# A two-layer graph attention kernel: the target's own row enters the early sums in the first stage, and the shared last blocks get four buffers

## The chip, the cores and the metric

The kernel runs on one core of one Trainium2 chip. The metric is the device time of one execution in microseconds; the kernel before has a median of 1749.48 us over 3 runs (1748.37 to 1754.7).

## What is computed

Two graph attention layers over the same sparse graph of 3327 nodes with 1024 features, each followed by a residual sum and a layer norm. Layer 0 has 8 heads of 128 columns, layer 1 has one head of 1024.

```python
# layer 0; layer 1 is the same with one head, its own W, and a relu on the result
h = (x @ W).reshape(C, H, D)
e = leaky_relu(alpha_src[:, :, None] + alpha_dst[:, None, :], 0.2)
attn = softmax(where(adj[None] == 0, -inf, e), axis=-1)
x = layernorm(x + einsum('hij,jhd->ihd', attn, h))
```

The adjacency is drawn with a density of 0.0024 and made symmetric, and every node is its own neighbour too. The weight exp(leaky_relu(s+d)) is computed as max(exp(0.8 s) exp(d), exp(0.2 d)); the factor exp(0.2 s) that is left out is the same for all edges of a target and falls out in the division. So a target row is a weighted sum of the rows of its neighbours, divided by the sum of the weights. The node's own edge is handled apart from the listed neighbours.

## The kernel before

**Tiles and tables.** The nodes make 26 tiles of 128 targets (NT = 26). The first stage multiplies x by W0 tile by tile and stores a table `h0_d` in memory: for each node 8 heads of 129 columns (128 and a one, which gathers the sum of weights: 1032 columns, DW) and 16 columns of exponentials (1048 in all, HW0). Beside the matmuls it turns the adjacency into lists of edges: masks come in as bytes (`ads`, three buffers), `count` and `words` count and pack them, `listing` finds the columns and writes `idx` and `tgt`, the source and target of each edge. The edges of a target tile are laid out in 17 lists of 128: blocks 0 and 1 of four lists each hold sources in the first 13 tiles, blocks 2 and 3 the others, and block 4 (EB) one list that all groups share, the "shared last block".

**The first stage's second half.** From tile 13 on a generator `sums_so_far` (L675) runs between the matmuls. It takes the first 20 target tiles (EARLY = 20) and does for each the sums over blocks 0 and 1 alone. For a block it fetches four lists with indirect transfers issued by POOL (`fetch`, L691) into one of three buffers (`near`, `near`, `far`), computes `w` and the weights `e` on VectorE (L708 to L712) and adds 64 small matmuls into PSUM (L721). After both blocks ScalarE copies the three PSUM banks to `z` (L764) and SyncE stores them as `half_d[s]` (L765).

**What orders the first stage.** Everything is scheduled by hand. The projection calls `pace()` after every two k-steps (12 slots for a tile of x); each slot lets `counting`, `listing` and `sums_so_far` take their next steps. The instructions stand in each engine's queue in the order in which the program emits them. In `sums_so_far` the weights of the next block are emitted ahead of the copy of the banks (L764).

**Layer 0 (the second stage).** `Layer0` items follow: 20 early targets with the blocks 2, 3 and 4 and 6 late ones with 0 to 4, in the order 20, 0 to 4, 21, 5 to 9 and so on. `prepare` (L1072, L1075) loads the node's own row `own` from `h0_d` and, for early targets, the stored sums `half`. `own` (L1081 to L1083) computes the own edge's weight on VectorE, `scale_own` (L1090) multiplies the own row by it with 8 ScalarE instructions, and `sums` (L1121) adds `own` and `half` to PSUM by matmuls with the identity, three for each row. `gather` (L1032) takes its buffers from two free lists: five for blocks of four lists and two (`ends`) for the shared last blocks. The requests stand in one fixed order, and `send` stops at the first one that has no free buffer.

**Layer 1 (the third stage).** `Target` items gather rows of `y_d` in the same way, sum them (L1234), turn the result (`finish`, tile `xT`) and multiply it by W1 (L1266).

Of the kernel before, what the change touches and what calls it, by code (L numbers as in the profile page):

```python
# [9 lines left out]
F32 = mybir.dt.float32  # L10
BF16 = mybir.dt.bfloat16
U8 = mybir.dt.uint8
I32 = mybir.dt.int32
# [13 lines left out]
def kernel(  # L27
# [111 lines left out]

    def by_head(row):  # L140
        return row[:, :DW].rearrange("p (h d) -> p h d", h=H)

    class Rows:

# [390 lines left out]
    with ExitStack() as own, tc.manual_schedule():  # L535
# [16 lines left out]

        def load_mask(t):
            if t < NT:
                ads[t] = masks[t % 3]
                if t == NT - 1:
                    nc.vector.memset(ads[t].bitcast(I32), 0)
                    nc.vector.memset(ads[t][:, :1], 1.0)
                for r in pieces(t):
                    nc.gpsimd.dma_start(ads[t][r, :N], adj[at(t, r), :])  # L560
# [114 lines left out]

        def sums_so_far():

            acc = part.bank("L", [P, 3, HALF], "part")
            acc = acc[:, :, : 3 * DH1].rearrange("p n (h d) -> p n h d", h=3)
            src = [near[0], near[1], far]  # L680
            k = EARLY * HB % 3
            src = src[-k:] + src[:-k] if k else src
            bound = nc.gpsimd.to_reg(THR - 1)

            def fetch(n):
                s, b = divmod(n, HB)
                if s > EARLY:
                    return
                for g in range(NG):
                    k = b * NG + g  # L690
                    nc.gpsimd.indirect_dma_start(  # L691
                        out=src[n % 3][:, g, :], out_offset=None, in_=h0_d[:THR, :],
                        in_offset=bass.IndirectOffsetOnAxis(ap=idx[:, s, k : k + 1], axis=0),
                        bounds_check=bound, oob_is_err=False,
                    )

            def marks(s):
                oh = part.sbuf("oh", [P, HB * NG, GT], 2)
                nc.vector.tensor_tensor(
                    oh, io_t[:, :GT].unsqueeze(1).to_broadcast([P, HB * NG, GT]),  # L700
                    tgt[:, s, : HB * NG].unsqueeze(2).to_broadcast([P, HB * NG, GT]), OP.is_equal,
                )
                return oh

            def weights(val, b, re, oh):
                blk = slice(b * NG, (b + 1) * NG)
                w = part.sbuf("w", [P, NG, H], 4)
                nc.vector.tensor_tensor(w, val[:, :, DW : DW + H], re[:, blk, :], OP.mult)  # L708
                nc.vector.tensor_tensor(w, w, val[:, :, DW + H :], OP.max)
                e = part.sbuf("e", [P, H * P], 2).rearrange("p (g h t) -> p g h t", g=NG, h=H)  # L710
                wide = [P, NG, H, GT]
                nc.vector.tensor_tensor(  # L712
                    e, oh[:, blk, :].unsqueeze(2).to_broadcast(wide), w.unsqueeze(3).to_broadcast(wide), OP.mult
                )
                return e

            def sums(acc, val, b, e, heads_):
                vals = val[:, :, :DW].rearrange("p g (h d) -> p g h d", h=H)
                for h in heads_:
                    for g in range(NG):  # L720
                        nc.tensor.matmul(  # L721
                            acc[g * GT : (g + 1) * GT, h // 3, h % 3, :], e[:, g, h, :], vals[:, g, h, :],
                            start=b == 0 and h in HEADS, stop=b == HB - 1 and h + 1 in HEADS,
                        )

            def listed(s):
                re = part.sbuf("re", [P, HB * NG, H], 3)
                nc.sync.dma_start(re, re_d[s][:, : HB * NG, :])
                return re

            res = [listed(0), listed(1)]
            for _ in range(3):
                yield
            for n in range(2):
                fetch(n)
                yield
                yield
                yield
            oh = marks(0)
            fetch(2)  # L740
            yield
            e = weights(src[0], 0, res[0], oh)
            yield
            for s in range(EARLY):
                for b in range(HB):
                    n = s * HB + b
                    val, last = src[n % 3], b == HB - 1
                    if n:
                        fetch(n + 2)
                    yield  # L750
                    if last and s + 1 < EARLY:
                        oh = marks(s + 1)
                    yield
                    sums(acc, val, b, e, range(H // 2))
                    yield
                    sums(acc, val, b, e, range(H // 2, H))
                    if last:
                        res.pop(0)
                    if n + 1 < EARLY * HB:
                        e = weights(src[(n + 1) % 3], (b + 1) % HB, res[0], oh)  # L760
                z = part.sbuf("z", [P, DW], 1)
                for n in range(3):
                    nh = HEADS[n + 1] - HEADS[n]
                    nc.scalar.activation(by_head(z)[:, HEADS[n] : HEADS[n + 1], :], acc[:, n, :nh, :], AF.Copy)  # L764
                nc.sync.dma_start(half_d[s], z)  # L765
                if s + 2 < EARLY:
                    res.append(listed(s + 2))
                yield

        wt = pool.tile([P, KT, WW], F32, bufs=1, name="wt")  # L770
        arow = [near[1][:1, 2 + n, :D] for n in range(2)]
# [12 lines left out]
        for n in range(4):  # L784
            half = slice(n % 2 * HALF, (n % 2 + 1) * HALF)
            nc.tensor.matmul(avs[:, n, :], one, arow[n // 2][:, half], start=True, stop=True)
        masks = [pool.tile([P, NP], U8, bufs=1, name=f"ad{n}") for n in range(3)]
        for ad in masks:
            nc.vector.memset(ad[:, N:], 0.0)
        junk = pool.tile([P, THR], U8, bufs=1, name="junk")  # L790
# [32 lines left out]
        score_column(7)  # L823
        opening.close()
        ph.more_banks(own, "late", {"S": 1})
        part.more_banks(own, "part", {"L": 1})
        ph.xp = bank("S", [P, EB, XS], "xp")
        ph.dd = ph.xp[:, 0, NG * NX :]

# [49 lines left out]
        for t in range(3, NT):  # L879
            load_x(t + 3)  # L880
            if 4 <= t < 4 + KT:
                nc.sync.dma_start(wt1[:, t - 4, :], w1[(t - 4) * P : (t - 3) * P, :])
            if t == 12:
                n, own_a = NT - 1, pool.tile([P, NT], I32, bufs=1, name="own")
                nc.vector.memset(own_a[:, n:], 0)
                step, m = adj.ap[0][0] + 1, rows(n)
                nc.sync.dma_start(
                    own_a[:, :n], bass.AP(tensor=adj.tensor, offset=adj.offset, ap=[[step, P], [P * step, n]])
                )
                nc.sync.dma_start(  # L890
                    own_a[:m, n:], bass.AP(tensor=adj.tensor, offset=adj.offset + n * P * step, ap=[[step, m], [1, 1]])
                )
            if t == 11:
                ph.iota([P, P], [[1, P]], "io_t", base=1, dst=io_t)
            if t == 16:
                nc.gpsimd.tensor_copy(loop, own_a)
            if t in (9, 10):
                table, w = (h0_d, HW0) if t == 9 else (y_d, HW)
# [73 lines left out]
    def sparse(own):  # L972
# [1 line left out]
        pool, bank, sbuf = ph.pool, ph.bank, ph.sbuf  # L974
        NS = 5
        srcs = near + [pool.tile([P, NG, HG], F32, bufs=1, name=f"src{n}") for n in range(HB, NS)]
        ends = [pool.tile([P, 1, HG], F32, bufs=1, name=f"end{n}") for n in range(2)]
        r1 = Rows(pool, 1)
        grow = pool.tile([P, NT], F32, bufs=1, name="grow")
        grows = pool.tile([P, NT, H], F32, bufs=1, name="grows")  # L980
# [74 lines left out]
        class Layer0:  # L1055
# [10 lines left out]
            def prepare(self):  # L1066
# [2 lines left out]
                self.y = ys[self.n % 3]  # L1069
                load_rows(self.y[:, :D], x, self.t)  # L1070
                self.h = sbuf("own", [P, HW0], 2)
                nc.sync.dma_start(self.h, h0_d[self.t * P : (self.t + 1) * P, :HW0])  # L1072
                if self.t < EARLY:
                    self.half = sbuf("xT", [P, DW], 2, "half")
                    nc.sync.dma_start(self.half, half_d[self.t])  # L1075

            def own(self):

                t, h = self.t, self.h
                es = self.es = sbuf("es0", [P, H], 2)  # L1080
                nc.vector.tensor_tensor(es, grows[:, t, :], h[:, DW : DW + H], OP.mult)  # L1081
                nc.vector.tensor_tensor(es, es, h[:, DW + H :], OP.max)
# [2 lines left out]
            def scale_own(self):  # L1085

                h = self.h
                for n in range(H):
                    d = slice(n * DH1, (n + 1) * DH1)
                    nc.scalar.activation(h[:, d], h[:, d], AF.Copy, scale=self.es[:, n : n + 1])  # L1090

# [22 lines left out]
            def sums(self, b):  # L1114
# [1 line left out]
                rowsof = self.src.pop(b)[:, :, :DW].rearrange("p g (h d) -> p g h d", h=H)  # L1116
                j = self.blocks.index(b)
                for n in self.banks.get(j, ()):
                    for row in (self.h, self.half) if self.t < EARLY else (self.h,):
                        part = row[:, HEADS[n] * DH1 : HEADS[n + 1] * DH1]  # L1120
                        nc.tensor.matmul(  # L1121
                            self.acc[n].rearrange("p h d -> p (h d)"), ident, part, start=False, stop=False
                        )
                if b == EB:
                    for h in range(H):
                        nc.tensor.matmul(
# [48 lines left out]
        class Target:  # L1175
# [80 lines left out]
            def finish(self):  # L1256

                t, z, res = self.t, self.z, self.res
                xT = sbuf("xT", [P, DW], 2)[:, :D].rearrange("p (k q) -> p k q", k=KT)
                yield from ph.transposed(xT, z, (0, 1))  # L1260
                o = sbuf("z", [P, D], 3, "o")
                for g in range(2):
# [283 lines left out]
```

## Time and profile before

| | |
|---|---|
| median of 3 runs | 1749.48 us |
| the profiled execution | 1751.44 us, its span 1749.6 us |
| TensorE, VectorE, ScalarE, GpSimd busy | 86%, 65%, 28%, 60% |
| transfers | 596.13 MB, mean 341 GB/s |
| first stage, up to the last projection matmul | to 563 us |
| first to last copy of the early sums (L764) | 274.8 to 562.9 us |
| layer 0 | to about 1060 us |
| layer 1 | to the end |

PE is TensorE, PEld its weight loads, DVE VectorE, ACT ScalarE, POOL GpSimd, SP SyncE. The page of the profile gives totals and 40 slices of 43.7 us. Other views give a stretch of time in numbers: busy us of each engine (with its instructions), the TensorE clock granted as a share of full speed, the mean busy share of the 16 DMA engines (it can exceed 1, because packets overlap), and GB/s. A wait is put down to what came last. A matmul in float32 leaves two records.

### The profile page before, as it was taken

The numbers are of one execution on the slowest core, as the hardware profiler recorded it, in microseconds if no ns is written. First come the engines' busy times: TensorE is split into PE (matmuls) and PEld (weight loads), VectorE is DVE, ScalarE is ACT, GpSimd is POOL, SyncE is SP. The second block draws the span as 40 slices with busy tenths as digits, with TensorE's granted clock in tenths as the row PEclk, the third lists the DMA queues.
The fourth block names the chain that finished last, engine by engine and source line by source line (L and its number), as shares of the span: only waits on it lengthen the run. The fifth ranks groups of instructions, "written<-read, shape, count | busy, mean of one in ns | idle before, by whom it ended". The sixth has DMA issues, their size and how long they took to land.

```text
span 1749.6 us, 34204 instructions
## 1 busy us (share of the span) xinstructions
PE 1497.3 (86%) x12755; PEld 865.2 (49%) x12755; DVE 1143.2 (65%) x3126; ACT 494.6 (28%) x1424; POOL 1050.7 (60%) x1309
## 2 busy tenths in 40 slices
PE   9799989898998477676676664799999999999998
PEld 5566655565665355555555542344444444444443
DVE  6799998888886788676877765344444453444443
ACT  5677752232323133332332322011111011111110
POOL 5433155776775666555656666677667766676750
PEclk9999999999999699887888886899999999999999
DMA  7688988999999999999999999999999999999980
GB/s 186 123 157 164 185 232 305 316 388 348 360 346 355 371 410 412 398 396 384 396 396 386 390 384 383 359 401 393 396 399 386 394 392 387 388 394 410 386 336 36
DMA packets 190321, 596.13 MB, mean 341 GB/s; under 512 B 37914, under 2 KB 47924, under 8 KB 190146
## 3 DMA queue, kind: packets, MB, share of 16 engines
q0 software_dynamic: 131056, 459.23, 73.4%
q1 hardware_dynamic: 58932, 134.36, 20.5%
q8 instruction: 103, 1.69, 0.4%
q14 instruction: 72, 0.59, 0.1%
q10 hardware_dynamic: 158, 0.26, 0.0%
HBM read 593.70 MB, written 54.99 MB: 371 GB/s over the span
## 4 chain that ended last, share of the span: by engine, by line
PE 41%; DMA 17%; DVE 5%; issue 2%; POOL 1%; ACT 0%; DVEq 0%; SPq 0%; ACTq 0%; POOLq 0%
PE mm L1266 22%; PE acc L1234 13%; DMA src<-h_d,idx 7%; DMA own<-h_d 4%; PE acc L1134 3%; DMA near<-h_d,idx 2%; PE acc L1121 2%; DMA src<-y_d,idx 2%; DVE e L1108 2%; PE tr L203 1%; DVE pr L998 1%; DVE y L1151 1%; DMA end<-h_d,idx 1%; DMA av<-in_L_gnn_a_dram 1%; DMA half<-half_d 0%
## 5 line engine op out<-in xcount | busy, mean ns | idle before, releaser
L571 PE MATMUL mm<-wt,xT 128*128 128x384 f32 (+1 forms) x1248 | 415.3, 478 | 0.4 <-DMA xT<-in_x_t_dram 0.4
L1266 PE MATMUL mm<-wt,xT 128*128 128x512 f32 x832 | 387.6, 604 | 0.0
L1032 POOL DMA_INDIRECT src<-y_d,idx x248 | 251.4, 1014 | 122.6 <-PE acc L1234 48.2
L571 PEld LDWEIGHTS mm<-wt,xT 128*128 128x128 f32 x1248 | 230.7, 195 | 130.2 <-issue 36.0
L1266 PEld LDWEIGHTS mm<-wt,xT 128*128 128x128 f32 x832 | 149.7, 189 | 198.9 <-issue 194.0
L1269 DVE SCALAR_TENSOR_TENSOR o<-mm,y 128x512 f32<-128x512 f32 x52 | 35.9, 691 | 317.3 <-PE mm L1266 317.3
L1032 POOL DMA_INDIRECT src<-h_d,idx x152 | 160.2, 1054 | 108.3 <-PE acc L1134 24.8
L1032 POOL DMA_INDIRECT near<-y_d,idx x168 | 171.1, 1018 | 65.7 <-issue 21.7
L1134 PE MATMUL acc<-src,e 128*32 128x129 f32 x2432 | 103.4, 340 | 74.6 <-DVE e L1108 74.6
L691 POOL DMA_INDIRECT near<-h_d,idx x112 | 124.1, 1108 | 51.5 <-issue 23.9
L1032 POOL DMA_INDIRECT near<-h_d,idx x96 | 103.3, 1076 | 75.5 <-DMA src<-h_d,idx 28.6
L1234 PE MATMUL acc<-src,es 128*32 128x341 f32 x1488 | 124.8, 470 | 26.0 <-DVE es L1225 26.0
L1134 PEld LDWEIGHTS acc<-src,e 128*32 128x32 f32 x2432 | 86.8, 138 | 92.6 <-DVE e L1108 81.2
L1248 ACT ACTIVATE z<-y,ri 128x342 f32<-128x342 f32 (+1 forms) x78 | 39.5, 569 | 299.1 <-DVE ri L1244 299.1
L1134 PE MATMUL acc<-near,e 128*32 128x129 f32 x1664 | 68.8, 332 | 58.6 <-DVE e L1108 44.2
L1108 DVE TENSOR_TENSOR e<-oh,way 128x1024 f32<-128x1024 f32 x90 | 109.9, 1221 | 7.9 <-PE acc L1134 0.6
L206 ACT ACTIVATE xT<-tr 128x512 f32<-128x512 f32 x52 | 31.0, 597 | 236.0 <-PE tr L203 236.0
L1134 PEld LDWEIGHTS acc<-near,e 128*32 128x32 f32 x1664 | 57.8, 134 | 70.7 <-DVE e L1108 48.6
L1234 PEld LDWEIGHTS acc<-src,es 128*32 128x32 f32 x1488 | 43.1, 112 | 96.3 <-issue 43.9
L1121 PE MATMUL acc<-own,ident 128*128 128x387 f32 (+1 forms) x156 | 72.0, 547 | 16.7 <-ACT own L1090 16.7
L411 ACT ACTIVATE junk<-ad 128x1664 uint8<-128x1664 uint8 x52 | 83.0, 1595 | 7.6 <-POOL ad L400 6.1
L1234 PE MATMUL acc<-near,es 128*32 128x342 f32 (+1 forms) x1008 | 82.0, 458 | 1.5 <-DVE es L1225 1.5
(225 smaller groups left out, 2378.7 us busy)
## 6 DMA issues: line engine op xcount, KB each, us to landing
own<-h_d SPq DMA_DIRECT2D x26, 524.0 KB
y_d<-y SPq DMA_DIRECT2D x26, 514.0 KB
y<-y_d SPq DMA_DIRECT2D x26, 514.0 KB
xT<-in_x_t_dram SPq DMA_DIRECT2D x26, 512.0 KB
h_d<-ht SPq DMA_DIRECT2D x25, 524.0 KB
y<-in_x_dram SPq DMA_DIRECT2D x25, 512.0 KB
out_dram<-o SPq DMA_DIRECT2D x25, 512.0 KB
ad<-in_adj_dram POOLq DMA_DIRECT2D x25, 415.9 KB
```

Of the source, the lines that this page charges most:

```text
L206: nc.scalar.activation(part, tr, AF.Copy)
L411: nc.scalar.activation(junk, ad[:, n * THR : (n + 1) * THR], AF.Copy, accum_out=self.d[:, n : n + 1])
L571: nc.tensor.matmul(accs[t, c], xT[t][:, k, :], wt[:, k, CUTS0[c] : CUTS0[c + 1]], start=k == 0, stop=k == KT - 1)
L691: nc.gpsimd.indirect_dma_start(out=src[n % 3][:, g, :], out_offset=None, in_=h0_d[:THR, :], in_offset=bass.IndirectOffsetOnAxis(ap=idx[:, ...
L1032: nc.gpsimd.indirect_dma_start(out=s[:, g, :w], out_offset=None, in_=table[:n, :], in_offset=bass.IndirectOffsetOnAxis(ap=idx[:, t, b * NG ...
L1108: nc.vector.tensor_tensor(e, oh.unsqueeze(2).to_broadcast([P, ng, H, wide]), wp.unsqueeze(3).to_broadcast([P, ng, H, wide]), OP.mult,)
L1121: nc.tensor.matmul(self.acc[n].rearrange("p h d -> p (h d)"), ident, part, start=False, stop=False)
L1134: nc.tensor.matmul(self.acc[h // 3][g * GT : (g + 1) * GT, h % 3, :], e[:, g, h, :], rowsof[:, g, h, :], start=j == 0 and h in HEADS, stop ...
L1234: nc.tensor.matmul(self.acc[c][to, :m], es[:, g, :], s[:, g, CUTS[c] : CUTS[c + 1]], start=b == 0, stop=b == EB,)
L1248: nc.scalar.activation(z[:, cut], self.res[:, cut], AF.Copy, scale=ri[:, 1:2])
L1266: nc.tensor.matmul(acc, xT[:, k, :], wt1[:, k, half], start=k == 0, stop=k == KT - 1)
L1269: nc.vector.scalar_tensor_tensor(o[:, half], acc, 0.0, res[:, half], op0=OP.max, op1=OP.add)
```

## The change

The early sums take in the target's own row in the first stage. The weights of the own edges are computed there (`own_terms`), each own row is loaded from `h0_d` through ScalarE's queue (`own_row`), scaled by 8 ScalarE instructions (`scale`), and three VectorE additions (`settle`) put the PSUM banks on top of it in place of ScalarE's copies. SyncE stores the sum two slots into the next target (`store`). The three row buffers are a new tile and two stretches of the mask buffers, so all counting is completed first (`need(NT - 1)`); the masks become one tile, and the adjacency's diagonal (`own_a`, `loop`) is loaded and converted earlier. PSUM for the early sums is three single banks in place of one tile of three. In layer 0 an early target loads `half_d` alone and leaves out the weight, the scaling and one of the two sets of identity matmuls. The shared last blocks have four buffers, the two new ones cleared by GpSimd, and `finish` of layer 1 uses the buffers of `own`.

```diff
+    own_e = const.tile([P, EARLY, H], F32, name="own_e")
...
-                ads[t] = masks[t % 3]
+                ads[t] = masks[(t + 1) % 3]
...
+            def own_terms(lo, hi):
...
+                for n, scale in enumerate((1.0, SLOPE)):
+                    nc.scalar.activation(mids[n], sd0[:, lo:hi, 1, :], AF.Exp, scale=scale)
+                nc.scalar.activation(e, sd0[:, lo:hi, 0, :], AF.Exp, scale=1 - SLOPE)
+                nc.vector.tensor_tensor(e, e, mids[0], OP.mult)
+                nc.vector.tensor_tensor(e, e, mids[1], OP.max)
+                nc.vector.tensor_tensor(e, e, loop[:, lo:hi].unsqueeze(2).to_broadcast([P, hi - lo, H]), OP.mult)
+
+            def own_row(s):
+                if s < EARLY:
+                    nc.scalar.dma_start(own_rows[s % 3], h0_d[s * P : (s + 1) * P, :DW])
+
+            def scale(s, heads_):
+                for h in heads_:
+                    d = by_head(own_rows[s % 3])[:, h, :]
+                    nc.scalar.activation(d, d, AF.Copy, scale=own_e[:, s, h : h + 1])
+
+            def settle(s, acc, n):
+                d = by_head(own_rows[s % 3])[:, HEADS[n] : HEADS[n + 1], :]
+                nc.vector.tensor_tensor(d, acc[n], d, OP.add)
+
+            def store(s):
+                nc.sync.dma_start(half_d[s], own_rows[s % 3])
+
             res = [listed(0), listed(1)]
             for _ in range(3):
                 yield
+            own_terms(0, NTH)
...
+            need(NT - 1)
+            own_rows.append(part.sbuf("z", [P, DW], 1, "own"))
+            own_row(0)
+            own_row(1)
             oh = marks(0)
             fetch(2)
...
             for s in range(EARLY):
+                acc = [part.bank("L", [P, HEADS[n + 1] - HEADS[n], DH1], "part") for n in range(3)]
                 for b in range(HB):
...
                     yield
+                    if s and b == 0:
+                        store(s - 1)
                     sums(acc, val, b, e, range(H // 2))
+                    scale(s, range(b * H // 2, b * H // 2 + 2))
                     yield
                     sums(acc, val, b, e, range(H // 2, H))
...
                         e = weights(src[(n + 1) % 3], (b + 1) % HB, res[0], oh)
-                z = part.sbuf("z", [P, DW], 1)
+                    scale(s, range(b * H // 2 + 2, (b + 1) * H // 2))
+                    if last:
+                        own_row(s + 2)
+                if s == NTH - 1:
+                    assert scored.issuperset(range(EARLY))
+                    own_terms(NTH, EARLY)
                 for n in range(3):
-                    nh = HEADS[n + 1] - HEADS[n]
-                    nc.scalar.activation(by_head(z)[:, HEADS[n] : HEADS[n + 1], :], acc[:, n, :nh, :], AF.Copy)
-                nc.sync.dma_start(half_d[s], z)
+                    settle(s, acc, n)
                 if s + 2 < EARLY:
                     res.append(listed(s + 2))
                 yield
+            store(EARLY - 1)
...
-        masks = [pool.tile([P, NP], U8, bufs=1, name=f"ad{n}") for n in range(3)]
+        ad = pool.tile([P, 3, NP], U8, bufs=1, name="ad")
+        masks = [ad[:, n, :] for n in range(3)]
+        own_rows = [ad.rearrange("p a b -> p (a b)").bitcast(F32)[:, n * HW0 : n * HW0 + DW] for n in range(2)]
...
-        part.more_banks(own, "part", {"L": 1})
+        part.more_banks(own, "part", {"L": 3})
...
-            if t == 12:
+            if t == 5:
                 n, own_a = NT - 1, pool.tile([P, NT], I32, bufs=1, name="own")
...
-            if t == 16:
+            if t == 11:
                 nc.gpsimd.tensor_copy(loop, own_a)
...
-        ends = [pool.tile([P, 1, HG], F32, bufs=1, name=f"end{n}") for n in range(2)]
+        ends = [pool.tile([P, 1, HG], F32, bufs=1, name=f"end{n}") for n in range(4)]
+        for end in ends[2:]:
+            nc.gpsimd.memset(end, 0.0)
...
                 self.h = sbuf("own", [P, HW0], 2)
-                nc.sync.dma_start(self.h, h0_d[self.t * P : (self.t + 1) * P, :HW0])
                 if self.t < EARLY:
-                    self.half = sbuf("xT", [P, DW], 2, "half")
-                    nc.sync.dma_start(self.half, half_d[self.t])
+                    nc.sync.dma_start(self.h[:, :DW], half_d[self.t])
+                else:
+                    nc.sync.dma_start(self.h, h0_d[self.t * P : (self.t + 1) * P, :HW0])
...
                 t, h = self.t, self.h
+                if t < EARLY:
+                    return
...
-                for n in range(H):
+                for n in range(H if self.t >= EARLY else 0):
...
-                    for row in (self.h, self.half) if self.t < EARLY else (self.h,):
-                        part = row[:, HEADS[n] * DH1 : HEADS[n + 1] * DH1]
...
+                    part = self.h[:, HEADS[n] * DH1 : HEADS[n + 1] * DH1]
+                    nc.tensor.matmul(self.acc[n].rearrange("p h d -> p (h d)"), ident, part, start=False, stop=False)
...
-                xT = sbuf("xT", [P, DW], 2)[:, :D].rearrange("p (k q) -> p k q", k=KT)
+                xT = sbuf("own", [P, HW0], 2, "xT")[:, :D].rearrange("p (k q) -> p k q", k=KT)
```

More of the change, by code (lines that the diff above doesn't have):

```diff
@@ L676, in sums_so_far @@
         def sums_so_far():
-            acc = part.bank("L", [P, 3, HALF], "part")
-            acc = acc[:, :, : 3 * DH1].rearrange("p n (h d) -> p n h d", h=3)
             src = [near[0], near[1], far]
@@ L721, in sums @@
                         nc.tensor.matmul(
-                            acc[g * GT : (g + 1) * GT, h // 3, h % 3, :], e[:, g, h, :], vals[:, g, h, :],
+                            acc[h // 3][g * GT : (g + 1) * GT, h % 3, :], e[:, g, h, :], vals[:, g, h, :],
                             start=b == 0 and h in HEADS, stop=b == HB - 1 and h + 1 in HEADS,
@@ L729, in listed @@
                 return re
+            def own_terms(lo, hi):
+                mid = ph.sbuf("bits", [P, 8, KMAX], 1, dt=I32).rearrange("p a b -> p (a b)").bitcast(F32)
+                m, e = (hi - lo) * H, own_e[:, lo:hi, :]
+                mids = [mid[:, n * m : (n + 1) * m].rearrange("p (t h) -> p t h", h=H) for n in range(2)]
+                for n, scale in enumerate((1.0, SLOPE)):
[16 more added lines that the diff above has]
+                nc.sync.dma_start(half_d[s], own_rows[s % 3])
             res = [listed(0), listed(1)]
@@ L1118, in sums @@
                 for n in self.banks.get(j, ()):
-                    for row in (self.h, self.half) if self.t < EARLY else (self.h,):
-                        part = row[:, HEADS[n] * DH1 : HEADS[n + 1] * DH1]
-                        nc.tensor.matmul(
-                            self.acc[n].rearrange("p h d -> p (h d)"), ident, part, start=False, stop=False
-                        )
+                    part = self.h[:, HEADS[n] * DH1 : HEADS[n + 1] * DH1]
+                    nc.tensor.matmul(self.acc[n].rearrange("p h d -> p (h d)"), ident, part, start=False, stop=False)
                 if b == EB:
```

## The prediction, made before the changed kernel ran

> **What bounds the kernel now.** I read the slices first, to part the stages.
>
> ```profile
> PE   9799989898998477676676664799999999999998
> ...
> DVE  6799998888886788676877765344444453444443
> ...
> DMA  7688988999999999999999999999999999999980
> GB/s 186 123 157 164 185 232 305 316 388 348 360 346 355 371 410 412 398 396 384 396 396 386 390 384 383 359 401 393 396 399 386 394 392 387 388 394 410 386 336 36
> ```
>
> A slice is 43.7 us. Slices 0 to 12 are the first stage, 14 to 23 layer 0, from 25 on layer 1. In layer 1 PE is full; the change touches nothing there but two spare buffers. The transfers look full almost everywhere, so I asked for sums over the two stretches that the change works in (columns: us, then PE, PEld, DVE, ACT and POOL busy with instructions, granted clock, DMA share, GB/s):
>
> ```profile
> 275.00:566.00 291.00, 269.53 (x3183) 176.16 (x3181) 239.71 (x641) 89.26 (x353) 200.72 (x260) 0.97 0.96 354
> ...
> 612.00:1050.00 438.00, 302.03 (x4334) 230.84 (x4333) 328.36 (x859) 137.33 (x355) 264.58 (x250) 0.83 1.01 395
> ...
> 656.00:700.00 44.00, 31.12 (x513) 23.42 (x513) 37.12 (x100) 15.19 (x43) 26.61 (x25) 0.92 1.03 412
> ```
>
> Layer 0 is bound by transfers: share 1.01 over 438 us at 395 GB/s, near the 412 of its best part, while PE is busy 69%, VectorE 75%. The stretch of the early sums is no such case: PE 93%, VectorE 82%, transfers 0.96. There I read the waits of VectorE and one stall of PE (the timeline):
>
> ```profile
> DVE w L708 <- DMA near<-h_d,idx: 17.4, 12, 3.0
> DVE w L708 <- DMA far<-h_d,idx: 7.4, 6, 1.8
> DVE kq L518 <- ACT xs L505: 6.7, 6, 3.0
> ```
>
> ```profile
> 415.37 0.19 DVE L708 TENSOR_TENSOR w<-near,re 128x32 f32<-128x32 f32 x1 [0.53 <-DMA near<-h_d,idx]
> 415.89 1.23 DVE L712 TENSOR_TENSOR e<-oh,w 128x1024 f32<-128x1024 f32 x1
> ...
> 417.22 1.95 PE L721 MATMUL part<-near,e 128*32 128x129 f32 x32 [4.36 <-issue]
> ```
>
> PE begins 0.1 us after `e` ends (415.89 + 1.23): "issue" is here a wait for VectorE, which had waited for a gather. Going down the 40 blocks, PE begins its sums within 0.25 us of the end of `e` in 18; in the others `e` lies ready for 0.4 to 5.5 us. VectorE waits for gathers 18 times, 24.8 us. So PE and VectorE run side by side there with little slack.
>
> **The change, part by part.** The sum is made on the profiled execution, 1751.44 us (span 1749.6); the median of the runs, 1749.48, is 1.96 lower, and I take that off at the end.
>
> *Layer 0 loses transfers.* 20 loads of `own` go, 128 x 1048 x 4 bytes = 0.537 MB each, 10.73 MB; `half_d` moves as before. At 395 GB/s that is **27.2 us**. It is the whole gain only while transfers stay the bound: the next engine is VectorE, whose 328 us in 438 fall by 20 x (0.170 + 0.169 + 0.263) = 12 us (L1081 to L1083), so 316 in about 410. ACT loses 160 scalings of 0.388 us (62 us), PE 120 records of 0.461 us (L1121: 72.0 us for 156), 55 us. All three lie beside the transfers and count for nothing by themselves; the 13.9 us that VectorE waits there for `own` go too, but a gather is late next. *Four last-block buffers:* with two, a block freed after target i's third block can't be refilled, since the next request in order is the last block of i+2. Ten-microsecond windows of the stage drop to 309 to 380 GB/s eight times. At 410 GB/s throughout, its 173 MB less 10.7 would take 396 us (gain 42). Ends: 22 us (some of it lost to waits elsewhere) and 42; I take **30**, nearest to the plain byte count.
>
> *A rule against this.* The rows first: 412 GB/s above. The Trainium skill, "DMA: Bandwidth & Descriptors", section "Specifications", puts the limit of memory for a core at about 358 GB/s. By that the early sums' stretch, at 354, has no room, moving 10.6 MB into it costs 29.5 us, layer 0 gives 30.0, and the sum is nothing; the measured 412 speaks for room.
>
> *The first stage gets VectorE work.* A `settle` reads a bank of 387 or 258 columns. The nearest rows read PSUM and a tile too:
>
> ```profile
> L1269 DVE SCALAR_TENSOR_TENSOR o<-mm,y 128x512 f32<-128x512 f32 x52 | 35.9, 691 | 317.3 <-PE mm L1266 317.3
> ...
> L1151 DVE SCALAR_TENSOR_TENSOR y<-acc,ri,y 128x128 f32<-128x128 f32 x208 | 56.0, 342 | 0.0
> ```
>
> ```profile
> L764 ACT ACTIVATE z<-part 128x387 f32<-128x387 f32 (+1 forms) x60 | 23.2, 467 | 61.9 <-PE part L721 37.4 <-issue 24.5
> ```
>
> The slope is (691 - 342) / 384 = 0.91 ns a column, so 0.58 and 0.46 us, 1.6 us for a target, 32 us for 20. VectorE gives nothing in return: the copies that go (last line) were ScalarE's. They stand behind the next block's `e`, so PE, whose next sums need the banks, also waits for two of them (1.16 us) after that `e` where it has no slack. What is queued behind: the list work, then the second block's `e`. Going down the blocks with these rows (an `e` is late by what VectorE carries, less its gather wait, but a gather is late as PE was two blocks before; PE is late by that less the block's slack), PE ends 17 us late. Ends: nothing, if the list work moves into waits; 32, if all shows.
>
> *And transfers.* 20 rows of 0.528 MB, 10.6 MB; the stretch moves 354 x 291 = 103 MB, at 395 it could move 115. It fits, with a queue: a row ahead of a gather holds it 0.528 / 395 = 1.34 us. The same walk with all gathers later by 1.4 us gives 26 to 30, by 0.7 us 21 to 23. Ends 0 and 27 more; I take 0.7 us. The first stage pays **21 us** in all.
>
> *ScalarE* gets 8 scalings (3.1 us) for three copies (1.4): +1.7 us in a target, at 31% busy. Two waits are new. `own_row(s+2)` waits until `store(s-1)`, issued about five slots (10 us) before, has landed; own loads took 8.8 to 9.9 us on the chain of waits in layer 0. The scalings wait for a row asked for one target and two slots ahead, 19 us. Queued behind are the copies of the projection's banks (three banks, each 7.6 us of matmuls: cover for over 10 us) and `mvg`, for which PE waited 15.2 us in 6 places already. Ends: -9 us (ScalarE no longer stands for the sums, and `mvg` waited behind L764 9.2 us) and +30 (1.5 a target); I take 0. The Trainium skill's same page, "Issuing engines are not separate DMA queues", says that a second issuing engine saves only issue time; the page of the profile can't show this, since ScalarE's queue moved 0.26 MB.
>
> *Small parts.* `need(NT - 1)`: the last counting (L411) ended at 256.4 us, the first sums began at 255.87, so at most one tile's count (2 x 1.6 us on ACT, 0.6 on VectorE) comes earlier: +1. The first two own rows are asked for only then; PE may stand for them, 0 to 5 us, taken with the ends. `own_terms`, six small VectorE operations: +1. Two clears by GpSimd ahead of the first gathers of layer 0, 0.97 us each (L160, same width): +2, as transfers wait there. The diagonal at tile 5: its second transfer waited for a VectorE clear (SP stood from 215.0 to 220.3); behind it on SP are h_d stores and x loads three tiles ahead, which cover it; GpSimd's conversion at tile 11 comes six tiles after the load. Its cost: 0; uncovered, the 5 us once. The new order of the masks, the split banks, the late stores on SP (which waits for the stage's pace anyway) and `finish` in the buffers of `own` (free since layer 0): 0; if a store holds the x loads, their three tiles cover it. The shorter wait of layer 0 for `half`, 2.9 us, goes with the transfers.
>
> The sum: -30 + 21 + 4 = -5; ScalarE freed of its stands (up to 9 us), half taken: -4. Together **-9 us**, 1742.4 on the profiled execution, **1740.5** beside the median.
>
> **The rivals.**
> *The first stage takes it free.* For it: VectorE's 31 us of waits there, as much as it gets; transfers reach 410 in single windows. Against: 18 of 40 blocks without slack. Then -30 to -38 + 5: about 1720.
> *The bytes only change place.* For it: shares of 0.96 and 1.01, equal bytes in all; the extra buffers bring nothing. First stage 27, layer 0 -27, +4: about 1752.
> *Slower: the gather loop closes.* Place: free buffer, gather, `e`, settle, sums, with three buffers. The gather is later by 1.34 us for the own row and VectorE by 1.6, one after the other: 2.9 us a target, 59 us; with slack absorbing a quarter, 45. It decides from 1.7 us a target (34 us, what layer 0 and the small parts leave). For it: gathers are late in 18 blocks already. Against: the walk, where lateness of the two overlaps. -30 + 45 + 4 = +19: about 1768.
> *It doesn't do what it says:* layer 0 stays as it is because gathers alone set its pace (their POOL issue, 1.0 us busy and 0.3 idle). Against: the windows at 412. Priced within the two before.
>
> **How the numbers follow.** A measurement of this kernel can tell 0.5% (8.7 us) from no change. Forecast case, -20 to -1: 0.50, of which 0.27 lies beyond 0.5%; free: 0.16; change of place: 0.18, within; slower: 0.16. Faster 0.43, within 0.41, slower 0.16. The range takes in the free case and reaches to the middle of the slower one: 1719 to 1765.
>
> **What would show it.** Layer 0: span from first to last L1134 shorter by 25 to 40 us at 395 GB/s or more. First stage: the last projection matmul ends 21 us after 563; settle at 1.6 us a target; PE's sums wait after settle; VectorE's waits for gathers no shorter than 20 us. It is wrong if ScalarE stands at `own_row` or the scalings for more than 3 us a target with PE idle beside it, or if layer 0's rate falls with its bytes.

## The result and the profile after

The changed kernel takes 1733.85 us (median of 4 runs, 1731.46 to 1737.93) where the kernel before takes 1748.92 (median of 4): a ratio of 0.9905, with an interval of 0.9881 to 0.993, or 15 us less. Two later measurements gave 0.9914 (0.9889 to 0.9939) and 0.9907 (0.9888 to 0.9926). The forecast was 9 us less.

The profiled execution took 1737.93 us, its span 1735.9. Its slices, in the order of those shown of before:

```profile
PE   9799979889988576567666644999999999999998
...
DVE  6699999899997698686877855354444444444443
...
DMA  7699998999999999999999999999999999999980
GB/s 187 113 166 171 183 247 316 354 399 397 379 361 341 333 409 410 400 399 381 404 389 385 378 387 380 358 399 401 393 395 392 396 392 392 388 393 410 386 332 37
```

The early sums run in slices 6 to 12. Slices 7 to 9 moved 316, 388 and 348 GB/s before and move 354, 399 and 397 now; slice 12 fell from 355 to 341. The two stretches, and the best part of layer 0 (same columns as before):

```profile
275.00:566.00 291.00, 259.22 (x3029) 169.25 (x3021) 258.39 (x679) 106.27 (x427) 188.50 (x250) 0.95 0.98 370
612.00:1050.00 438.00, 279.12 (x4420) 215.01 (x4420) 337.61 (x850) 96.61 (x213) 285.09 (x266) 0.81 1.01 394
656.00:700.00 44.00, 29.25 (x452) 22.52 (x450) 33.74 (x83) 10.22 (x21) 27.40 (x26) 0.81 1.03 411
```

In the early sums' stretch VectorE went from 239.7 to 258.4 us busy and transfers from 354 to 370 GB/s; PE fell from 269.5 to 259.2, as the same work is spread over a longer time. Layer 0 is as full of transfers as before (394 GB/s, share 1.01). What VectorE and then PE wait for in the first stretch, and below that the waits of PE before:

```profile
DVE w L708 <- DMA near<-h_d,idx: 12.5, 7, 4.9
DVE kq L520 <- ACT xs L507: 3.3, 1, 3.3
DVE w L708 <- DMA far<-h_d,idx: 2.0, 1, 2.0
```

```profile
PE part L721 <- DVE e L712: 18.6, 10, 5.5
PE xp L493 <- ACT mvg L474: 6.6, 3, 5.3
PE part L721 <- DVE ad L754: 5.1, 3, 3.9
```

```profile
PE part L721 <- DVE e L712: 6.7, 9, 1.4
...
PE part L721 <- issue: 4.4, 1, 4.4
```

VectorE waits 14.5 us for gathers; it was 24.8. PE waits 18.6 us for `e`, where it waited 6.7 and the 4.4 that the prediction read as such a wait; the wait for the settles themselves, 5.1 us, comes on top. And the rows of the new work (by form):

```profile
L754 DVE TENSOR_TENSOR ad<-part,ad 128x387 f32<-128x387 f32 x28 | 14.5, 554 | 5.1 <-PE part L721 5.1
L754 DVE TENSOR_TENSOR own<-part,own 128x387 f32<-128x387 f32 x12 | 6.1, 553 | 0.0
L754 DVE TENSOR_TENSOR ad<-part,ad 128x258 f32<-128x258 f32 x14 | 5.9, 419 | 1.9 <-ACT ad L750 1.9
L754 DVE TENSOR_TENSOR own<-part,own 128x258 f32<-128x258 f32 x6 | 2.5, 418 | 0.0
```

Together 29.0 us of settles, 0.55 and 0.42 us each.

To see where the time went, I part every profile at two points that a tile's view gives: the last projection matmul (end of the first stage) and the first and last sums over a far block (layer 0). Of the changed kernel:

```profile
L573 PE MATMUL mm<-wt,xT x1248: 392/486/1010, 9.5 to 574.8; 128*128 128x384 f32 x120, 128*128 128x272 f32 x59
...
L1178 PE MATMUL acc<-src,e x2432: 270/275/424, 608.2 to 1052.6; 128*32 128x129 f32 x188
```

The same two groups of the kernel before:

```profile
L571 PE MATMUL mm<-wt,xT x1248: 392/486/1010, 9.5 to 563.1; 128*128 128x384 f32 x120, 128*128 128x272 f32 x59
...
L1134 PE MATMUL acc<-src,e x2432: 270/276/424, 595.9 to 1065.7; 128*32 128x129 f32 x188
```

The first stage's last matmul started at 574.8 us (before: 563.1), and layer 0 took 1052.6 - 608.2 = 444.4 us (before: 1065.7 - 595.9 = 469.8). From there to the end it is 683.3 us, before 683.9. So in this pair of profiles layer 0 gave 25.4 us and the first stage took 11.7; the stretch between the two took 0.6 and the end gave 0.6 back.

### The profile page after: what moved, and what is told of

The parts are those of the page before. It is cut to its first block, busy times and chain, and to the rows that moved or that the text cites. A ratio compares the mean times of both kernels' runs of the same rounds, so it can differ in the third digit from the quotient of the medians.

```text
span 1735.9 us, 33973 instructions
## 1 busy us (share of the span) xinstructions
PE 1461.5 (84%) x12635; PEld 840.6 (48%) x12635; DVE 1159.6 (67%) x3132; ACT 472.7 (27%) x1370; POOL 1053.2 (61%) x1311
## 4 chain that ended last, share of the span: by engine, by line
PE 40%; DMA 12%; DVE 8%; issue 4%; POOL 1%; ACT 0%; DVEq 0%; SPq 0%; ACTq 0%; POOLq 0%
PE mm L1310 22%; PE acc L1278 13%; DMA src<-h_d,idx 4%; DMA near<-h_d,idx 3%; PE acc L1178 3%; DVE e L1155 2%; DMA src<-y_d,idx 1%; DVE y L1195 1%; PE tr L205 1%; DMA own<-h_d 1%; DVE pr L1043 1%; DVE st L226 1%; DMA near<-y_d,idx 1%; DVE y L233 1%; PE acc L1167 1%
## 5 line engine op out<-in xcount | busy, mean ns | idle before, releaser
L1077 POOL DMA_INDIRECT src<-h_d,idx x152 | 163.8, 1077 | 86.4 <-PE acc L1178 26.7
L1178 PE MATMUL acc<-src,e 128*32 128x129 f32 x2432 | 100.7, 333 | 70.8 <-DVE e L1155 70.8
L1178 PEld LDWEIGHTS acc<-src,e 128*32 128x32 f32 x2432 | 84.3, 134 | 88.7 <-DVE e L1155 77.6
L1178 PE MATMUL acc<-near,e 128*32 128x129 f32 x1664 | 70.9, 340 | 56.1 <-DVE e L1155 45.2
L1178 PEld LDWEIGHTS acc<-near,e 128*32 128x32 f32 x1664 | 59.7, 138 | 69.4 <-DVE e L1155 48.7
```

The lines of the kernel that those rows point to most:

```text
L1077: nc.gpsimd.indirect_dma_start(out=s[:, g, :w], out_offset=None, in_=table[:n, :], in_offset=bass.IndirectOffsetOnAxis(ap=idx[:, t, b * NG ...
L1178: nc.tensor.matmul(self.acc[h // 3][g * GT : (g + 1) * GT, h % 3, :], e[:, g, h, :], rowsof[:, g, h, :], start=j == 0 and h in HEADS, stop ...
```

## The experiments

The theories named in the expectations are told anew in each; in all of them the question is what paid in layer 0 (fewer bytes or more buffers) and what the first stage paid for (VectorE, transfers or ScalarE). The first group of runs was made on a chip on which the kernel before takes 1800.52 us; the second and third were made on chips where it takes 1752.35 and 1751.36.

### First group, on the slower chip: terms of the first stage, and two buffers

```diff
 # m_act
-                nc.vector.tensor_tensor(d, acc[n], d, OP.add)
+                nc.scalar.activation(d, acc[n], AF.Copy)
 # m_norow
-                if s < EARLY:
+                if s < 3:
                     nc.scalar.dma_start(own_rows[s % 3], h0_d[s * P : (s + 1) * P, :DW])
 # m_both: the two together
 # a_ends2
-        ends = [pool.tile([P, 1, HG], F32, bufs=1, name=f"end{n}") for n in range(4)]
-        for end in ends[2:]:
-            nc.gpsimd.memset(end, 0.0)
+        ends = [pool.tile([P, 1, HG], F32, bufs=1, name=f"end{n}") for n in range(2)]
```

> The changed kernel with the settle on ScalarE: a copy of the PSUM bank over the own row, as before, in place of VectorE's addition. It leaves the own edge of the 20 early targets out of layer 0's sums. Loads, scalings and layer 0 stay as in the changed kernel. Theory A (VectorE's 30 us of settles are what the first stage pays, transfers cost nothing): the last projection matmul ends at 563 to 567 us in place of 574.8, the median about 1723. Theory B (the own rows' transfers are what it pays, VectorE's work goes into waits for gathers): last projection matmul at 572 to 575, median 1732 to 1734.

> The changed kernel with own rows loaded for the first three early targets only; later targets scale and add to what lies in the row buffers, so layer 0's sums of the early targets are not the reference's. VectorE's settles and ScalarE's scalings stay. 17 loads of 0.528 MB (9.0 MB) leave the first stage. Theory A (VectorE): last projection matmul still at 572 to 575 us, median 1732 to 1734. Theory B (transfers): it ends at 563 to 567, median about 1723.

> The changed kernel with both taken away: ScalarE copies over the row, own rows loaded for the first three targets only; the own edge of the early targets is left out. What stays of the change: the scalings, the small parts, and layer 0 with one row and four last-block buffers. By both theories the first stage ends as before (last projection matmul at 563 to 566 us) and layer 0 keeps its gain of 25 us: median 1720 to 1724. If the sum of the two single gains is larger or smaller than this one, the two costs overlap or add.

> The changed kernel with two buffers for the shared last blocks, as before, and no clears. If the bytes alone make layer 0's gain (10.7 MB at 395 GB/s, 27 us), the time is that of the changed kernel within 2 us. If the deeper queue brings part of it (my prediction gave it 3 us, up to 15), it is 3 to 15 us slower and layer 0's rate falls below 394 GB/s.

The medians in us that I expected suppose the chip of the first profiles; on this one only the ratios to before, and runs with each other, can be compared.

| | median, us | ratio to before (interval) | last projection matmul | layer 0 | from there to the end |
|---|---|---|---|---|---|
| m_act | 1770.16 | 0.9841 (0.981 to 0.9872) | 576.7 | 455.6 | 702.2 |
| m_norow | 1765.34 | 0.9811 (0.9783 to 0.9839) | 568.4 | 451.3 | 702.5 |
| m_both | 1766.38 | 0.9825 (0.9797 to 0.9853) | 574.7 | 452.5 | 703.3 |
| a_ends2 | 1795.8 | 0.9977 (0.9955 to 0.9998) | 574.4 | 484.0 | 706.2 |

By theory A of the first stage m_act, which lacks VectorE's settles, was to end it at 563 to 567. It ends at 576.7, no earlier than with the settles (a_ends2 has the changed first stage: 574.4). This does not refute the theory. m_both, which both theories put at 563 to 566, ends at 574.7, while m_norow, which has the settles, ends at 568.4: copies by ScalarE behind its scalings seem to cost about as much as the settles, so m_act and m_both do not take the cost away. The medians of m_both and m_norow differ by 1 us. Single profiles are not enough to price terms of this size.

a_ends2 shows something that I had not foreseen: layer 0 is about 30 us longer with two buffers than in the three others, whose layer 0 is that of the changed kernel. GpSimd's waits between 620 and 1040 us, of a_ends2:

```profile
POOL end L1075 <- PE acc L1168: 36.0, 8, 5.7
POOL end L1075 <- DVE ri L1188: 31.3, 6, 6.7
```

and of m_act, its longest wait at a last block:

```profile
POOL end L1077 <- issue: 6.7, 21, 0.6
```

With two buffers GpSimd stands 67 us at the requests of the last blocks, and behind them the next gathers: layer 0's transfers (612 to 1040 us) fall from 391 (m_act) to 366 GB/s, share 0.97. Part of this standing has only moved there from other requests: all of GpSimd's waits in that stretch are 173 us, and 151 to 154 in the three others. The prediction had priced this loop over two buffers at 3 us.

The chip differs in more than its time. PE's waits at its sums in layer 0 between 612 and 1040 us (L1178; L1176 in a_ends2), of a_ends2, of m_act, and of after2 from the second group:

```profile
PE acc L1176 <- issue: 89.0, 247, 1.1
```

```profile
PE acc L1178 <- issue: 52.3, 132, 1.1
```

```profile
PE acc L1178 <- DVE e L1155: 112.1, 30, 5.6
```

The first two lines are PE standing at its sums in many short stops (at most 1.1 us) for which the profile names nothing that it waited for. On the other chips no profile has them there; PE waits for VectorE's `e`, which in a_ends2 it does for 1.2 us. In the early sums too (275 to 566 us) PE has 24 to 42 such stops here, 9 to 17 us in all, as much as the terms that these runs were to price. So the first stage is priced on the other chips, below.

### Second group: the bytes put back, and VectorE's work alone

```diff
 # a_own4 (from the changed kernel)
                     nc.sync.dma_start(self.h[:, :DW], half_d[self.t])
+                    spare = sbuf("z", [P, D], 3, "spare")
+                    nc.sync.dma_start(spare, h0_d[self.t * P : (self.t + 1) * P, :D])
 # b_dve (from the kernel before)
-                    nc.scalar.activation(by_head(z)[:, HEADS[n] : HEADS[n + 1], :], acc[:, n, :nh, :], AF.Copy)
+                    nc.vector.tensor_tensor(
+                        by_head(z)[:, HEADS[n] : HEADS[n + 1], :], acc[:, n, :nh, :],
+                        zero.unsqueeze(2).to_broadcast([P, nh, DH1]), OP.add,
+                    )
 # before2, after2: the two kernels as they are
```

> The kernel before, for a profile on the same chip as the three that follow. All theories: the last projection matmul ends at 563 to 567 us, layer 0 (first to last sums over a far block) takes 470 us or, where the chip's transfers are slower, up to 500.

> The changed kernel, for a profile and a time on the same chip. All theories: 14 to 18 us faster than before where transfers are as fast as in the first profiles; up to 30 faster where they are slower and layer 0 gains more. Last projection matmul at 574 to 575 us.

> The changed kernel with the own row of each early target loaded in layer 0 as well, 128 x 1024 columns (0.524 MB, 20 times) into a buffer that nobody reads: the bytes that the change took from layer 0 are back, the four last-block buffers stay. Theory A, my prediction's (the bytes are the gain): layer 0 is 26 us longer than in the changed kernel, the median 24 to 28 us higher, that is about that of the kernel with two buffers or worse. Theory B (the four buffers are the gain, since two leave fetch buffers empty): layer 0 is at most 10 us longer.

> The kernel before with VectorE emptying the PSUM banks of the early sums (an addition of zero) in place of ScalarE's copies; nothing else changes and the result is the same. Theory A (VectorE's work is what the first stage pays): the first stage ends 10 us or more later (17 by my walk down the blocks), median 10 to 17 us above before. Theory B (it goes into VectorE's waits for gathers, and the stage pays for the own rows' transfers and ScalarE's scalings): within 4 us of before.

| | median, us | ratio to before (interval) | last projection matmul | layer 0 | from there to the end |
|---|---|---|---|---|---|
| before2 | 1757.77 (one run; before: 1752.35) | | 569.0 | 471.9 | 682.7 |
| after2 | 1736.88 | 0.9914 (0.9889 to 0.9939) | 568.8 | 445.5 | 684.5 |
| a_own4 | 1761.3 | 1.0052 (1.0036 to 1.0068) | 576.2 | 469.9 | 684.4 |
| b_dve | 1757.4 | 1.0026 (1.001 to 1.0041) | 568.5 | 470.4 | 684.5 |

On this chip the bytes decide. With 20 x 0.524 MB put back (10.5 of the 10.7 MB) layer 0 is 469.9 us, that of before within 2 us, though it keeps the four buffers and ScalarE, VectorE and PE have the relief of the change; the median is 24.4 us above after2, theory A's 24 to 28. Between 612 and 1040 us the stage moves, with the bytes and without them (a_own4, then after2):

```profile
612.00:1040.00 428.00, 272.62 (x4071) 209.48 (x4063) 317.04 (x798) 89.31 (x195) 258.11 (x243) 0.81 1.01 397
```

```profile
612.00:1040.00 428.00, 278.06 (x4314) 214.86 (x4317) 326.92 (x830) 94.49 (x209) 274.82 (x257) 0.80 1.01 393
```

The share is 1.01 in both and the rate the same to 1%: less to move, less time.

b_dve prices VectorE's work. It is 0.26% slower than before, 4.6 us (1.8 to 7.2): nearer to theory B's 4 than to theory A's 10 to 17. VectorE's waits between 275 and 566 us show where the work went, of before2 and then of b_dve:

```profile
DVE w L708 <- DMA near<-h_d,idx: 22.7, 11, 6.7
...
DVE w L708 <- DMA far<-h_d,idx: 6.5, 5, 1.7
```

```profile
DVE w L708 <- DMA near<-h_d,idx: 4.9, 5, 1.4
...
DVE w L708 <- DMA far<-h_d,idx: 1.2, 3, 0.6
```

Its 28.9 us of additions (20.5 and 8.4) took the place of waiting: 29.2 us of waits for gathers became 6.1. In this pair of profiles PE ends the sums of no block more than 1.6 us later in b_dve, and those of the last one 0.6 us earlier: no lateness builds up over the 40 blocks. (The two executions took 1757.77 and 1758.34 us, so the 4.6 us of the medians is not in this pair.)

### Third group: two buffers, rows and scalings on a chip as fast as that of the result

a_ends2b is the kernel a_ends2, m_norow2 is m_norow, after3 the changed kernel.

```diff
 # m_noscale
             def scale(s, heads_):
-                for h in heads_:
+                for h in ():
```

> The changed kernel with two last-block buffers again, where the transfers are as fast as in the profiles of before and after. Theory A (the bytes alone are the gain): within 3 us of the changed kernel, layer 0 at 445 us. Theory C (both are needed: with two buffers GpSimd stands at the requests of the last blocks, and the transfers run empty as soon as the own rows no longer fill them): layer 0 at 465 us or more, DMA share under 1, GpSimd standing 40 us or more at the last blocks, the median 15 to 30 us above the changed kernel, so about that of before.

> As m_norow (own rows loaded for three early targets only), with the changed kernel beside it in the same call. If the rows' transfers cost the first stage something, it is 4 to 8 us faster than the changed kernel; if the rows fit into gaps, within 3 us.

> The changed kernel with ScalarE's 160 scalings of the own rows left out, so that the own edges of the early targets count with weight one. If ScalarE's 62 us of scalings delay the copies and lists on which PE and VectorE wait, it is 4 us or more faster than the changed kernel; if they lie in ScalarE's idle time (my prediction: 0), within 3 us.

> The changed kernel, beside the three others in the same call: 0.989 to 0.993 of before.

| | median, us | ratio to before (interval) | last projection matmul | layer 0 | from there to the end |
|---|---|---|---|---|---|
| a_ends2b | 1737.68 | 0.9921 (0.9904 to 0.9938) | 573.8 | 445.1 | 685.4 |
| m_norow2 | 1731.98 | 0.9881 (0.9862 to 0.9901) | 571.9 | 445.1 | 682.4 |
| m_noscale | 1734.47 | 0.9909 (0.989 to 0.9927) | 571.7 | 443.0 | 682.7 |
| after3 | 1736.43 | 0.9907 (0.9888 to 0.9926) | 575.6 | 442.2 | 682.1 |

Here the number of buffers makes 1.3 us, which is nothing that can be told, and GpSimd's longest group of waits at a last block is

```profile
POOL end L1075 <- PE acc L1176: 3.1, 6, 1.5
```

where it was 36.0 and 31.3 us on the other chip. So theory A holds on this chip. On that one the signs of theory C were there (layer 0 484.0 us, share 0.97, GpSimd standing 67 us), though the changed kernel itself was not run on it. The own rows' transfers cost the first stage some 4.4 us (17 of the 20 rows, m_norow2 beside after3; the intervals overlap, so this is likely rather than sure). On the slower chip m_both beside m_act, which differ in the same rows, gives 3.8, again with intervals that overlap. The scalings cost 2 us by the medians, which the intervals don't tell from nothing.

## Why the prediction was right in the direction and short by 6 us

**In the sum.** Layer 0 gave 26.5 us where 30 were put, and the first stage took about 9 where 21 were put. The two errors have opposite signs in the sum, so that the total came out nearer than the larger of them, 12 us; that part is luck.

**Layer 0: right, the added 3 us were not there.** The plain byte count was 27.2 us; four profiles of the kernels without the bytes and with four buffers (after, after2, after3, m_norow2) give 442.2 to 445.5 us, three with the old layer 0 (before, before2, b_dve) 469.8 to 471.9, a difference of about 26.5. The 3 us added for the deeper queue did not show on these chips (a_ends2b). "Layer 0's rate of 395 or more" was 394. The next bound named, VectorE, did not come up: it is busy 337.6 us of 438.

**The first stage: 21 us predicted, about 9 measured in all.** The 21 are 17 for VectorE and 4 for transfers by the walk down the blocks; the small parts (+4) and ScalarE's freedom (-4) cancel. This is the term that was mis-sized. a_own4 has everything of the change but the bytes taken from layer 0 (all but 0.24 MB of them), and is 1.0052 of before: 9.1 us (6.3 to 11.9) is what the rest of the change costs. Single executions scatter by more than a term (last projection matmul of the unchanged first stage 563.1 and 569.0; of the changed one 574.8, 568.8, 575.6, 576.2, 573.8 on the chips of this speed), which is why the price is read from medians.

- *VectorE, 17 us by the walk:* 4.6 (b_dve). The duration was well bounded (1.6 us a target from the nearest rows, measured 1.52), and PE's direct wait for settled banks was there as forecast (5.1 us). The step that failed is the rule of the walk that "a gather is late as PE was two blocks before": it made every gather wait form again behind PE. In the runs the gathers came early enough for VectorE's added work to go into the waits, 23 of 29 us in b_dve, as the rival "the first stage takes it free" had argued. The profile of before already spoke against the rule. There are three buffers (`src[n % 3]`), so a gather's request needs the end of PE's sums three blocks before; 37 of 38 requests were issued before PE had ended the sums two blocks before. Only 11 of 37 followed the end three blocks before at once (0.25 us); the others came 0.6 to 7.9 us after it, so something else set their time. That this accounts for the whole difference is argued and not shown. What was to show the step right, waits for gathers "no shorter than 20 us", measured 14.5. (PE begins within 0.25 us of the end of `e` in 17 blocks of before, not 18, which changes nothing.)
- *Transfers, 4 us:* 4.4 (m_norow2), likely as sized. VectorE's waits for gathers are 10.8 us in m_norow2 and 16.3 in after3 on the same chip, which fits own rows that hold up gathers; but the profiles of the changed kernel alone spread from 10.9 (after2) to 16.3.
- *ScalarE, 0 with ends far apart, and -4 for its freedom:* -4 cannot be told apart, since b_dve frees ScalarE of its copies too: its 4.6 us stands against 17 - 4 = 13. The two new waits cost nothing: `own_row` found its store landed each time, and the scalings waited once, 1.2 us, for the first row. Of ScalarE's new events in the changed kernel:

```profile
L745 ACTq EVENT_SEMAPHORE  x18: 17/17/38, 250.2 to 520.7; - x18
```

The longest of these 18 waits is 38 ns.

- *Small parts, 4 us:* from the last projection matmul to the first far sums it is 32.5 to 33.1 us in three profiles without the clears (before, before2, b_dve) and 33.1 to 34.8 in three of the changed kernel: about 1 us for the two clears, where 2 were put, with a scatter as large. b_dve's 4.6 and the rows' 4.4 make up a_own4's 9.1, so little seems left for `need` and `own_terms`; each of the three figures is uncertain by some 3 us.

The rule of the Trainium skill that was weighed, a limit of about 358 GB/s ("DMA: Bandwidth & Descriptors", "Specifications"), would have made the sum nothing by the prediction's estimate from it. The stretch that had 354 GB/s moves 370 now, and slices 8 and 9 reach 399 and 397: the measurement decides against it here. The same page's rule that a second issuing engine has no transfer engines of its own ("Issuing engines are not separate DMA queues") was not tested: no run here put the own rows on another queue.

**What stays open.** Why two last-block buffers cost 30 us on the chip of the first group and nothing on that of the third. The changed kernel itself did not run on that chip; its layer 0 was seen there in m_act, m_norow and m_both, and the kernel before has no profile there, so what the bytes alone gave is not known either. Slower transfers are a weak reason: between 612 and 1040 us the three move 391 to 393 GB/s at shares of 1.01 and 1.02, where after2 and after3 move 393 and 395. PE's stops are the larger difference. The last blocks in a_ends2 wait for PE's sums (L1168) and for the VectorE step behind them (L1188), so a PE that falls behind holds the two buffers longer; this is an argument, and no run here tests it. What stops PE, the traces do not show. In layer 1 both show: the part after layer 0 takes 702 to 706 us there in place of 682 to 685, with transfers at 381 GB/s and a share of 1.00 in m_act between 1150 and 1700 us (before2: 394 at 1.01; after2: 382 at 0.98), and with stops inside PE's sums.

## What to carry to other kernels

In a stage whose transfers are full (share 1.0 over the whole of it), count its bytes: taking away 10.7 MB gave 26.5 us at 395 GB/s, and putting them back took it all away, whatever the engines beside it had been spared. Bytes moved to a stage with room cost little there (likely 4 us), and an engine's added work in a coupled pair of engines can be paid from its own waits (23 of 29 us here), so ask how far ahead its inputs were requested before the work is called late. A buffer that brings nothing on one chip can be worth 30 us on another: price it on more than one.

## What the runs showed of the hardware that was not expected

- One chip took 1800.52 us for the kernel before, where others took 1748.92 to 1752.35, with a granted TensorE clock no lower (0.938 to 0.947 in the profiles there, 0.918 to 0.927 in the others).
- On that chip PE makes short stops that the profile puts down to no other engine: 52 to 89 us in all at the sums of layer 0 between 612 and 1040 us, where the other chips show none. In layer 1 (1150 to 1700 us) a group of 24 records of sums of 341 columns took 1.93 us in all 87 groups seen of after2, and up to 2.76 us in m_act, with 16 of 78 above 2.2.
- A VectorE addition of a PSUM bank and a tile takes 0.55 us for 128x387 and 0.42 for 128x258, 1.05 ns a column; the slope taken from two other rows was 0.91.
- A load of an own row on ScalarE's queue was issued 5.2 to 13.6 us after the store of its buffer on SyncE's, and never stood for it (longest stand 38 ns), though own loads in layer 0 took 8.8 to 9.9 us on the chain of waits before.
